# The ssm residual of blocks 2 to 6 by a second Strassen level, with LayerNorm's last small operations on VectorE and w2's second fold from SBUF

## The chip, the core and the metric

One core of a Trainium2 chip runs the kernel. The metric is the device time of one launch in microseconds (us); for the kernel before it is the median of three runs. The engines are TensorE (PE, with its weight loads as PEld), VectorE (DVE), ScalarE (ACT), GpSimd (POOL) and the sync engine (SP), which issues most of the DMAs.

## The reference

```python
emb = jnp.dot(jax.nn.silu(t), ada_w) + ada_b
shift_msa, scale_msa, gate_msa, shift_mlp, scale_mlp, gate_mlp = jnp.split(emb, 6, axis=-1)
norm = _ln(x) * (1.0 + scale_msa[:, None]) + shift_msa[:, None]
h = jax.nn.gelu(jnp.dot(norm, ssm_w1) + ssm_b1, approximate=False)
x = x + gate_msa[:, None] * (jnp.dot(h, ssm_w2) + ssm_b2)
norm2 = _ln(x) * (1.0 + scale_mlp[:, None]) + shift_mlp[:, None]
hf = jax.nn.gelu(jnp.dot(norm2, ff_w1) + ff_b1, approximate=True)
x = x + gate_mlp[:, None] * (jnp.dot(hf, ff_w2) + ff_b2)
```

x is (2, 2048, 512) in float32, t is (2, 512), ssm_w1 and ssm_w2 are 512 x 512, ff_w1 is 512 x 1024 and ff_w2 is 1024 x 512.

## The kernel before

x is cut into eight blocks of 512 tokens, four to each of the two batches. A block goes through LayerNorm 1 (`n1`), the product with ssm_w1 (hA), the product with ssm_w2 that is added to x (oA), LayerNorm 2 (`n2`), the product with ff_w1 (hC) and the product with ff_w2 that is added to x (oC). All weights stay in SBUF. The gates are multiplied into the columns of w2 and fw2 (a "fold"), once for each batch; for the second batch the weights are loaded again and folded again, while the kernel runs.

Every product is made by a fast scheme with fewer multiplications. hA and oA use Strassen's seven products P1 to P7; each is made of four matmuls of 128 x 128 by 256 columns and has a bank of PSUM: P1, P6, P7, P4 the bank "y", P2 "x", P5 and P3 "v". Sums of inputs that a product needs are made ahead on POOL. oC (`residual_in_leaves`, L761) carries Strassen one level further: P1 and P6 are plain products of eight matmuls, the others are cut into leaves, and a round R0 to R6 has ten matmuls of 128 columns, of leaf number n of five products. hC uses a scheme of its own (`products`, L955), whose inputs are 20 sums (`HK_B`, L915) made on POOL into the tile `forms`.

What a product adds to x, DVE adds from PSUM (L739 for oA, L789 and L838 for oC); for hidden layers L701 and L1002 are the like. A bank is used again and again, so an add that is late holds back the product that comes next in its bank. Where the next leaf value goes to the bank "x" too, ACT copies it there after R0 (L858 to L861).

LayerNorm takes statistics on DVE (L512, L513), then `scales` (L544) makes from mean and variance 1/sqrt (`pow`, on POOL, L550) and the scale and shift (`rstd`, `nmr`), by eight operations of 4 elements a partition on POOL. With them ACT writes the normalized rows (`normal`, L580), DVE transposes blocks of 32 (`turn`, L591), DMAs move the blocks (`move`, L600), and ACT scales and shifts (`moved`, L623).

The order on every engine is the order in the program: a product or round has hooks, and operations hung to a hook are issued right behind it. The loop over i = 1 to 7 issues, for i up to 4, hC_i, oA_(i+1), oC_i, hA_(i+2); for i = 5 (`ahead`) hC_5, oA_6, hA_7, oC_5, oA_7; then hC_6, oC_6, hC_7, oC_7. So the LayerNorm between oA_(i+1) and hC_(i+1) runs while oC_i is on PE, and n1 of block i + 2 runs while hC_i is on PE. The sums for oC_i (`sums24`, `sums35`, `sums7`, from L1023) are made on POOL during oA_(i+1) and at the start of oC_i. `leaf_fold` (i = 1 and 4) are sums of fw2 on DVE in oC. `refold2` (i = 2) reloads w2 in oC_2 and folds it in hA_4, with the gate that ACT copied to PSUM; `refold5` (i = 3) does the same with fw2.

The names that the steps of the prediction touch: `residual` L723, `residual_in_leaves` L761, `scales` L544, `weight_of_second` L391, `sums_of_first` L350 and `sums_of_second` L359 (four operations, all recorded at L348), `take_gate` L333, `load_gate` L328, `apart_leaves` L452, `gate_bias` L898.

Of the kernel before, what the change touches and what calls it, by code (L numbers as in the profile page):

```python
# [140 lines left out]
def kernel(  # L141
# [249 lines left out]
    def weight_of_second(w_sb, s, gt, engs, cut=1):  # L391
# [15 lines left out]
        return second_operands(q, s), ops + sums_of_second(q, s, nc.gpsimd, cut)  # L407
# [22 lines left out]

    Q = P // C
# [67 lines left out]
    class Norm:  # L499
# [44 lines left out]
        def scales(self, on_dve=False):  # L544

            n, v = self.name, nc.gpsimd
            ve = small.tile([P, C], F32, tag="ve", name=f"ve{n}")
            v.tensor_scalar(ve, self.mv[:, :, 1], self.of_squares, EPS, ALU.mult, ALU.add)
            r = small.tile([P, C], F32, tag="r", name=f"r{n}")
            v.tensor_tensor(r, ve, minus_half, ALU.pow)  # L550
            e = small.tile([P, C], F32, tag="e", name=f"e{n}")
            self.rstd = small.tile([P, C], F32, tag="rstd", name=f"rstd{n}")
            self.nmr = small.tile([P, C], F32, tag="nmr", name=f"nmr{n}")
            if on_dve:
                v = nc.vector
                v.tensor_tensor(e, r, ve, ALU.mult)
                v.scalar_tensor_tensor(e, e, -0.5, r, ALU.mult, ALU.mult)
                v.scalar_tensor_tensor(self.rstd, e, 1.5, r, ALU.add, ALU.mult)
                v.scalar_tensor_tensor(self.nmr, self.mv[:, :, 0], -1.0, self.rstd, ALU.mult, ALU.mult)
# [6 lines left out]
            v.tensor_scalar(self.nmr, self.nmr, -1.0, None, ALU.mult)  # L566
# [188 lines left out]

    LEAVES = ("P1", "P2", "P6", "P5", "P7", "P3", "P4")
# [737 lines left out]
```

## Time and profile before

| | |
|---|---|
| median of three runs | 586.56 us (586.24 to 586.59) |
| span of the profiled execution | 584.7 us |
| PE busy in the span | 577.8 us (99%) |
| DVE, ACT, POOL busy | 416.3, 263.2 and 428.2 us (71, 45 and 73%) |
| oA_3 on PE (223.10 to 235.18) | 12.1 us |
| oC_2 on PE (235.18 to 257.72) | 22.5 us |

A row of the timeline has the start in us from the span's start, the length in us, the engine, the line, the operation, out <- in with shapes and the number of instructions; in brackets stands the idle time of the engine before it and what ended it. A row of the groups ends with the busy time in us, the mean ns of one and the idle time before. A row of windows has the busy time of each engine in one stretch. The rows themselves stand in the prediction.

### The profile page before, as it was taken

How to read it: one execution, taken by the hardware profiler on the slowest of the kernel's cores; microseconds unless marked ns; L12 is line 12 of the kernel's file. 1: busy time of each engine (PE TensorE's matmuls, PEld its weight loads, DVE VectorE, ACT ScalarE, POOL GpSimd, SP SyncE). 2: the span in 40 equal slices, each digit the busy share in tenths (PEclk: the TensorE clock that was granted, in tenths of full speed). 3: DMA queues.
4: the chain of work that ended last, by engine and by line, in shares of the span. 5: the costliest groups of instructions: out<-in, count | busy, mean ns of one | idle time of the engine just before them, and what ended most of it. 6: DMA issues, size and time to landing. Idle time of an engine off the chain costs nothing.

```text
span 584.7 us, 9487 instructions
## 1 busy us (share of the span) xinstructions
PE 577.8 (99%) x3303; PEld 515.5 (88%) x3303; DVE 416.3 (71%) x752; ACT 263.2 (45%) x479; POOL 428.2 (73%) x518
## 2 busy tenths in 40 slices
PE   8999999999999999999999999999999999999997
PEld 4888888888889888998889988898888998899896
DVE  4978788987968375685756856884756367787676
ACT  2234357405642555435742588226673331731420
POOL 2875359999997938969788799998679445369351
PEclk9999999999999999999999999999999999999999
DMA  8990322303205403372043820244130330031002
GB/s 317 396 394 11 91 64 79 112 36 108 56 19 166 142 1 72 107 218 73 2 91 71 290 73 22 52 84 154 52 73 0 112 107 1 1 73 72 2 1 72
DMA packets 25243, 56.49 MB, mean 97 GB/s; under 512 B 4672, under 2 KB 5740, under 8 KB 23532
## 3 DMA queue, kind: packets, MB, share of 16 engines
q1 hardware_dynamic: 21856, 51.67, 27.9%
q10 hardware_dynamic: 3340, 4.22, 2.9%
q8 instruction: 26, 0.43, 0.3%
q14 instruction: 21, 0.17, 0.1%
HBM read 32.80 MB, written 8.40 MB: 70 GB/s over the span
## 4 chain that ended last, share of the span: by engine, by line
PE 93%; DMA 3%; DVE 2%; issue 0%; DVEq 0%
PE px_hC L985 10%; PE py_oA L475 9%; PE py_hA L475 9%; PE py_hC L985 8%; PE py_oC L778 8%; PE pv_hC L985 8%; PE pl_oC_P_y L824 8%; PE pv_oA L475 5%; PE pl_oC_P_v L824 5%; PE pv_hA L475 4%; PE pl_oC_P_x L824 3%; PE py_oC L475 2%; PE py_hC L475 2%; PE px_oA L475 2%; DMA ada<-in_L_cond_ada_w_dram 2%; PE px_hA L475 2%
## 5 line engine op out<-in xcount | busy, mean ns | idle before, releaser
L348 POOL TENSOR_TENSOR hSC<-hClo,hChi 128x512 f32<-128x512 f32 (+1 forms) x16 | 19.7, 1236 | 39.6 <-ACT hChi L980 34.2
L623 ACT ACTIVATE nT<-nT,mod,mod 128x512 f32<-128x512 f32 x32 | 23.4, 803 | 55.4 <-DMA nT<-blocks 39.8
L512 DVE BATCH_NORM_STATS2 st<-x 128x6 f32<-128x512 f32 x60 | 40.6, 678 | 5.4 <-DMA x<-in_x_dram 5.1
L923 POOL TENSOR_TENSOR forms<-forms 128x256 f32<-128x256 f32 x56 | 41.8, 747 | 3.3
L985 PE MATMUL py_hC<-forms,fw 128*128 128x256 f32 x168 | 41.0, 380 | 0.0
L1002 DVE TENSOR_TENSOR hClo<-hClo,py_hC 128x512 f32<-128x512 f32 x42 | 28.6, 684 | 15.3 <-ACT hClo L999 9.4
L985 PEld LDWEIGHTS py_hC<-forms,fw 128*128 128x128 f32 x168 | 31.7, 190 | 4.7 <-ACT hChi L999 0.2
L591 DVE STREAM_TRANSPOSE blocks<-nT 128x512 f32<-128x512 f32 x32 | 22.2, 705 | 13.5 <-ACT nT L580 13.5
L923 POOL TENSOR_TENSOR forms<-nT,forms 128x256 f32<-128x256 f32 x42 | 30.5, 748 | 1.7 <-PE pl_oC_P_v L824 1.3
L623 ACT ACTIVATE x<-x,mod,mod 128x512 f32<-128x512 f32 x24 | 17.6, 802 | 31.6 <-DMA x<-blocks 31.6
L923 POOL TENSOR_TENSOR forms<-nT 128x256 f32<-128x256 f32 x14 | 10.4, 741 | 28.4 <-ACT nT L623 18.0
L1002 DVE TENSOR_TENSOR hChi<-hChi,pv_hC 128x512 f32<-128x512 f32 x35 | 23.3, 681 | 10.4 <-PE pv_hC L985 6.7
L580 ACT ACTIVATE nT<-x,nmr,rstd 128x512 f32<-128x512 f32 x32 | 24.1, 806 | 13.3 <-POOL nmr L566 13.3
L985 PE MATMUL px_hC<-forms,fw 128*128 128x256 f32 x112 | 27.6, 379 | 0.0
L980 ACT ACTIVATE hClo<-hClo,colsT 128x256 f32<-128x256 f32 x56 | 25.3, 500 | 5.0 <-DVE hClo L1002 4.8
L838 DVE TENSOR_TENSOR x<-pl_oC_P_y,x 128x256 f32<-128x256 f32 (+1 forms) x66 | 24.7, 375 | 3.0 <-PE pl_oC_P_y L824 1.2
L475 PE MATMUL py_oA<-w,hA 128*128 128x256 f32 x112 | 26.5, 379 | 0.0
L999 ACT ACTIVATE hChi<-py_hC 128x512 f32<-128x512 f32 x14 | 7.6, 593 | 41.2 <-PE py_hC L985 41.0
L980 ACT ACTIVATE hChi<-hChi,colsT 128x256 f32<-128x256 f32 x56 | 25.1, 497 | 1.9 <-DVE hChi L1002 1.9
L739 DVE TENSOR_TENSOR x<-py_oA,x 128x512 f32<-128x512 f32 x26 | 17.8, 686 | 11.2 <-PE py_oA L475 10.6
L778 PE MATMUL py_oC<-fw_s,hSC 128*128 128x256 f32 x112 | 25.3, 379 | 0.0
L778 PE MATMUL py_oC<-fw,hClo 128*128 128x256 f32 x112 | 25.3, 379 | 0.0
(339 smaller groups left out, 1781.1 us busy)
## 6 DMA issues: line engine op xcount, KB each, us to landing
x<-in_x_dram SPq DMA_DIRECT2D x13, 1024.0 KB
out_dram<-x SPq DMA_DIRECT2D x14, 512.0 KB
ada<-in_L_cond_ada_w_dram SPq DMA_DIRECT2D x6, 1024.0 KB
x<-blocks SPq DMA_DIRECT2D x96, 64.0 KB
nT<-blocks SPq DMA_DIRECT2D x80, 64.0 KB
fw<-in_L_cond_ff_w_dram SPq DMA_DIRECT2D x2, 2048.0 KB
w<-in_L_cond_ssm_w_dram SPq DMA_DIRECT2D x3, 1024.0 KB
nT<-blocks ACTq DMA_DIRECT2D x48, 64.0 KB
```

The lines of the kernel that those rows point to most:

```text
L475: nc.tensor.matmul(ps[b][j * apart][:, j, :], lhs(p, j, k), rhs(p, j, k), start=(fresh and j * (not apart) == 0 and k == 0), stop=(p in (" ...
L512: nc.vector.bn_stats(st, xs[self.i][:, c, :])
L580: nc.scalar.activation(t, x_c, AF.Identity, bias=self.nmr[:, c : c + 1], scale=self.rstd[:, c : c + 1])
L591: nc.vector.transpose(self.bl[:, :, :, c, :].rearrange("p m k q -> p k m q"), self.nT[:, c, :].rearrange("p (k m q) -> p k m q", k=KD, m=C),)
L623: nc.scalar.activation(dst, src, AF.Identity, bias=shift, scale=scale)
L778: yield lambda j=j, k=k: nc.tensor.matmul(ps[BANK[p]][:, j, :], hops(p, j, k), wops[p][:, k, :], start=False, stop=(k == kdim - 1), skip_g ...
L824: nc.tensor.matmul(t[:, n, :], hops.leaves[p][f][:, k, :], leaf_wops[p][f][:, k, :], start=room not in started, stop=(f in ("P2", "P3", "P ...
L838: nc.vector.tensor_tensor(d, src, d, ALU.add)
L923: eng.tensor_tensor(reg[d], reg[a], reg[b], ALU.add if f == "+" else ALU.subtract)
L980: nc.scalar.activation(h, h, AF.Gelu_apprx_tanh, bias=fb1T[:, m : m + 1])
L985: nc.tensor.matmul(ps[b][:, j, :], fa[ra][:, j * P : (j + 1) * P], fb[rb].rearrange("p a (c q) -> p c a q", q=Q), start=(fresh and j == 0) ...
L1002: nc.vector.tensor_tensor(dest(d), dest(d), ps[b], op)
```

## The change

1. `residual_with_leaves` takes the place of `residual` for oA_2 to oA_6. P1, P5, P6 and P7 stay plain; P2, P3 and P4 are made in seven rounds of three matmuls 128 x 128 by 128 columns, in the order P1 R0 P5 R1 R2 P6 R3 R4 P7 R5 R6. Every plain product and every round but R0 is followed by its adds to x.
2. The sums that the leaves need: `leaf_sums` of hA (eight operations on POOL, at step 10 of hC) and `leaves_of_w2` (eight on POOL, ahead of the loop, and again at hA_4's P4). oA_7 takes the old form; `plain_w2` (two operations on DVE) gives it back its operands.
3. `scales` is cut in `root` and `rest`. For four early LayerNorms all stays on POOL. For the others `ve` and the four last operations are made on DVE, and `pow` alone on POOL. `root` and `rest` are hung to oC's P1 (n2), and to steps 2 and 12 of hC (n1; 0 and 9 at i = 1, 7 and 12 at i = 4, 0 and 2 at i = 5).
4. On POOL, sums24 is halved in oA; behind `pow` come the halves of sums35, sums7 and sums24 in turn.
5. w2's second fold reads the gate from a row in SBUF; four operations run in oC_2, four in hA_4, and its sums on DVE in place of POOL. The gate's copy in PSUM, for the bias alone, is taken at hA_4's P5. The loads of the gates are hung to oA in place of hC's first step, and `store_gates(2)` to hA_1's P7.
6. Tiles share memory: `w2_t` holds the identity matrix, silu and the gate rows early and the leaf sums of w2 later; the leaf sums of hA lie in a part of `forms`; `leaf_row` has two rows in place of three and two copies on ACT in place of one.

The diff, cut:

```diff
-    def weight_of_second(w_sb, s, gt, engs, cut=1):
+    def weight_of_second(w_sb, s, gt, engs, cut=1, sum_eng=nc.gpsimd):
...
+    def leaves_of_w2(w_sb, s, eng):
+
+        def views(w, n):
+            v = w.rearrange("p h (q e d) -> p h q e d", e=2, d=P)
+            return {f"{h + 1}{e + 1}": v[:, h, :, e] for h in range(2) for e in range(2)}
+
+        t23 = thirds(w2_t[:, : 6 * P].rearrange("p (s q d) -> p s q d", s=3, q=2))
+        t4 = thirds(w2_t[:, 6 * P :].rearrange("p (s q d) -> p s q d", s=3, q=1))
+        q23, q4 = views(w_sb[:, KD // 2 :, :], 2), views(s[:, 2], 1)
...
+        return ops, sums_of_second(q23, t23, eng) + sums_of_second(q4, t4, eng)
...
-        def scales(self, on_dve=False):
...
+        def scales(self):
+            self.root()
+            self.rest()
+
+        def root(self):
...
+            self.early = self.i + self.which in (2, 3)
+            v = nc.gpsimd if self.early else nc.vector
...
+            v.tensor_scalar(self.ve, self.mv[:, :, 1], self.of_squares, EPS, ALU.mult, ALU.add)
+            nc.gpsimd.tensor_tensor(self.r, self.ve, minus_half, ALU.pow)
+
+        def rest(self):
...
+            v = nc.vector
+            v.tensor_tensor(e, r, ve, ALU.mult)
+            v.scalar_tensor_tensor(e, e, -0.5, r, ALU.mult, ALU.mult)
+            v.scalar_tensor_tensor(self.rstd, e, 1.5, r, ALU.add, ALU.mult)
+            v.scalar_tensor_tensor(self.nmr, self.mv[:, :, 0], -1.0, self.rstd, ALU.mult, ALU.mult)
...
+    STEPS = ("P1", "R0", "P5", "R1", "R2", "P6", "R3", "R4", "P7", "R5", "R6")
+    STEP_OF = {"P1": "P1", "P2": "P5", "P6": "P6", "P5": "R4", "P7": "P7", "P3": "R5", "P4": "R6"}
+
+    def residual_with_leaves(name, i, hops, wops, leaf_wops, hooks):
...
+        def plain(p):
...
+            d = plain_dests[p]
+            nc.vector.tensor_tensor(d, ps[BANK[p]].unsqueeze(2).to_broadcast(d.shape), d, ALU.add)
+
+        def leaf_round(r):
+            f = LEAVES[r]
+            b = LEAF_BANK[f]
+            for n, p in enumerate(("P2", "P3", "P4")):
+                nc.tensor.matmul(
+                    rooms[b][:, n, :],
+                    hops.leaves[p][f],
+                    leaf_wops[p][f],
+                    start=b not in started,
+                    stop=(f in ("P2", "P3", "P4")),
+                    skip_group_check=True,
+                )
+                started.add(b)
+            if r == 0:
+                nc.scalar.copy(rooms["x"][:, :3], rooms["y"][:, :3])
+                started.add("x")
+                return
+            t, e = LEAF_AT[f]
+            for d, n in ((X[:, 0, t, :, e, :], slice(0, 2)), (X[:, 1, t, :1, e, :], slice(2, 3))):
+                nc.vector.tensor_tensor(d, rooms[b][:, n], d, ALU.add)
...
+        def leaf_sums(self, eng):
...
+            return sums_of_first(q24, s24, eng) + sums_of_first(q3, s3, eng)
...
-            hook(hooks, (0,), [n1[i + 2].scales])
+            hook(hooks, (0,), [n1[i + 2].root])
+            hook(hooks, (9,), [n1[i + 2].rest])
...
+            hook(hooks, (10,), hA[i + 1].leaf_sums(nc.gpsimd))
...
-            hook(hooks, (1,) if ahead else (7,) if unread_stats else (5,), [n1[i + 2].scales])
+            hook(hooks, (0,) if ahead else (7,) if unread_stats else (2,), [n1[i + 2].root])
+            hook(hooks, (2,) if ahead else (12,), [n1[i + 2].rest])
...
-            hook(hooks, ("P5",), sums24)
-        if fold:
-            sums35 = sums35[:2] + sums7[:2] + sums35[2:] + sums7[2:]
-        elif nx2:
-            hook(hooks, ("P7",), sums7)
+            hook(hooks, ("P5",), sums24[:2])
         if nx2:
...
+            sums35 = sums35[:2] + sums7[:2] + sums24[2:] + sums7[2:] + sums35[2:]
...
-            residual(f"oA_{i + 1}", i + 1, hA[i + 1], w2_ops, KD // 2, hooks, order=CARRIED)
...
+            residual_with_leaves(f"oA_{i + 1}", i + 1, hA[i + 1], w2_ops, w2_leaf, hooks)
...
-            if leaf_fold:
-                hook(hooks, ("P1",), leaf_fold[:2])
-            hook(hooks, ("P1",), [lambda: n2[i + 1].scales()])
+            hook(hooks, ("P1",), [lambda: n2[i + 1].root()])
+            hook(hooks, ("P1",), (leaf_fold or [])[:2] + [lambda: n2[i + 1].rest()])
             hook(hooks, ("P1",), sums35)
...
+            w2_ops, w2_fold = weight_of_second(w2_sb, w2_s, gate_rows[2, b], (nc.vector,), sum_eng=nc.vector)
+            hook(hooks, ("R2", "R4", "R4", "P3"), w2_fold[:KD])
...
-            take_gate(2, b)
-            w2_ops, w2_fold = weight_of_second(w2_sb, w2_s, gate[2, b], (nc.vector,))
-            hook(hooks, ALL, [multiply_2] + w2_fold)
...
+            hook(hooks, ("P1", "P1", "P2", "P6"), w2_fold[KD:])
+            hook(hooks, ("P5", "P4"), [lambda: found.update(gb2=bias_2()), lambda: found["gb2"]()])
+            w2_leaf, ops = leaves_of_w2(w2_sb, w2_s, nc.gpsimd)
+            hook(hooks, ("P4",), ops)
...
+            plain_w2(w2_sb, w2_s, nc.vector)
             residual(f"oA_{i + 2}", i + 2, hA[i + 2], w2_ops, KD // 2, hooks, order=CARRIED)
```

More of the change, by code (lines that the diff above doesn't have):

```diff
@@ new lines, in rest @@
+        def rest(self):
+            n, ve, r = self.name, self.ve, self.r
+            e, self.rstd, self.nmr = [small.tile([P, C], F32, tag=t, name=f"{t}{n}") for t in ("e", "rstd", "nmr")]
+            if self.early:
+                v = nc.gpsimd
+                v.tensor_tensor(e, r, r, ALU.mult)
+                v.tensor_tensor(e, e, ve, ALU.mult)
+                v.tensor_scalar(e, e, -0.5, 1.5, ALU.mult, ALU.add)
+                v.tensor_tensor(self.rstd, r, e, ALU.mult)
+                v.tensor_tensor(self.nmr, self.mv[:, :, 0], self.rstd, ALU.mult)
+                v.tensor_scalar(self.nmr, self.nmr, -1.0, None, ALU.mult)
+                return
+            v = nc.vector
[3 more added lines that the diff above has]
+            v.scalar_tensor_tensor(self.nmr, self.mv[:, :, 0], -1.0, self.rstd, ALU.mult, ALU.mult)
@@ L1274 @@
     fold = None
+    w2_leaf, ops = leaves_of_w2(w2_sb, w2_s, nc.gpsimd)
+    run(ops)
     later, unread_stats = [], []
```

144 lines of the change are left out of this document (90 added, 54 removed).

## The prediction

> **What bounds the kernel now.** I read the page from the top: busy time of the engines, then the chain that ended last.
>
> ```profile
> span 584.7 us, 9487 instructions
> PE 577.8 (99%) x3303; PEld 515.5 (88%) x3303; DVE 416.3 (71%) x752; ACT 263.2 (45%) x479; POOL 428.2 (73%) x518
> ...
> PE 93%; DMA 3%; DVE 2%; issue 0%; DVEq 0%
> ```
>
> PE is busy 99% of the span, and the chain of waits is PE for 93%. So two things move the time: matmul time that is added or taken away, and a new wait on PE. The profiled execution spans 584.7 us; the median of the runs is 586.56, so 1.86 us lie around the span, and I add that to every sum.
>
> The stretches of one regular block tell what the other engines have to spare (oA_3, oC_2, the most of hA_4; the last row is iteration i = 4 up to 406):
>
> ```profile
> core 0: us, PE busy (x) PEld busy (x) DVE busy (x) ACT busy (x) POOL busy (x), PEclk, DMA share, GB/s
> 223.26:235.35 12.09, 12.09 (x58) 10.64 (x57) 5.06 (x9) 4.60 (x11) 10.19 (x9) 1.00 0.42 101
> 235.35:257.88 22.53, 22.53 (x173) 21.70 (x173) 16.06 (x36) 9.62 (x16) 16.58 (x23) 1.00 0.50 146
> 257.88:268.25 10.37, 10.37 (x50) 9.13 (x49) 6.32 (x12) 5.01 (x9) 9.98 (x15) 1.00 0.39 126
> ...
> 337.00:406.00 69.00, 69.00 (x387) 62.13 (x387) 46.21 (x87) 38.95 (x79) 63.53 (x72) 1.00 0.27 77
> ```
>
> PE has no idle time there, and its granted clock (PEclk) is 1.00. The shares are of the stretch's own length. DVE has room in oA (5.06 of 12.09 us). POOL hasn't: 63.53 of 69.00 us in i = 4.
>
> **Part 1: P2, P3, P4 by leaves, on PE.** The chain of waits gives the cadence of both shapes.
>
> ```profile
> 154.10 1.73 PE py_oA L475 x8
> 175.33 2.23 PE pl_oC_P_x L824 x20
> ```
>
> A plain product is four matmuls of 256 columns in eight records: 1.73/4 = 0.432 us each. A leaf round in oC is ten matmuls of 128 columns in twenty records: 0.223 each. In each of oA_2 to oA_6, 12 matmuls of 256 (5.19 us) become 21 of 128 (4.69 us). That is 0.50 us less per block and 2.48 us in all: a span of 582.2 if PE waits for nothing new. oA then takes about 11.6 us in place of 12.09.
>
> **Part 2: more adds on DVE.** The groups of adds by shape:
>
> ```profile
> L739 DVE TENSOR_TENSOR x<-py_oA,x 128x512 f32<-128x512 f32 x26 | 17.8, 686 | 11.2 <-PE py_oA L475 10.6
> L838 DVE TENSOR_TENSOR x<-pl_oC_P_y,x 128x256 f32<-128x256 f32 x44 | 18.5, 420 | 1.6 <-DVE x L789 0.5
> L838 DVE TENSOR_TENSOR x<-pl_oC_P_y,x 128x128 f32<-128x128 f32 x22 | 6.2, 283 | 1.3 <-PE pl_oC_P_y L824 1.2
> 389.72 1.22 DVE L874 TENSOR_TENSOR x<-py_oC,x 128x1024 f32<-128x1024 f32 x1
> ...
> 235.18 3.62 PE L778 MATMUL py_oC<-fw,hClo 128*128 128x256 f32 x16
> ...
> 236.81 0.66 DVE L512 BATCH_NORM_STATS2 st<-x 128x6 f32<-128x512 f32 x1
> ...
> 237.61 0.66 DVE L512 BATCH_NORM_STATS2 st<-x 128x6 f32<-128x512 f32 x1
> ...
> 238.91 0.69 DVE L789 TENSOR_TENSOR x<-py_oC,x 128x512 f32<-128x512 f32 x1 [0.43 <-PE py_oC L778]
> ```
>
> Six adds of 512 (4.1 us) become two of 512, two of 1024 and six pairs of 256 and 128: 2 x 0.69 + 2 x 1.22 + 6 x 0.70 = 8.0 us. oA's 12.09 us hold the 3.9 us more, but the end of oA moves back on DVE. From T0, the start of oA: P7 ends at 11.60 - 2 x 0.67 = 10.26. An add starts 0.27 behind its product (oC_2's P1, two products long, ends at 235.18 + 3.46 = 238.64, its add starts at 238.91), so P7's runs from 10.53 to 11.75; the adds of R5 and R6 end at 13.15; the four statistics follow each other at 0.80 (236.81, 237.61) and end at 16.4; oC's P1 add ends at 17.0 and `ve`, now on DVE, at 17.2.
>
> **Part 3: the chain of LayerNorm.** In oC_2 before, with T0 = 223.10:
>
> ```profile
> 238.57 0.19 POOL L548 TENSOR_SCALAR ve<-mv 128x4 f32<-128x4 f32 x1 [0.61 <-DVE mv L513]
> 238.85 1.04 POOL L550 TENSOR_TENSOR r<-ve,minus_half 128x4 f32<-128x4 f32 x1
> 241.36 0.23 POOL L566 TENSOR_SCALAR nmr<-nmr 128x4 f32<-128x4 f32 x1
> 241.56 1.27 POOL L348 TENSOR_TENSOR forms<-hSC,hSC 128x512 f32<-128x512 f32 x1
> 241.62 1.52 ACT L580 ACTIVATE nT<-x,nmr,rstd 128x512 f32<-128x512 f32 x2 [3.92 <-POOL nmr L566]
> 243.05 0.36 ACT L858 COPY pl_oC_P_x<-pl_oC_P_y 128x256 f32<-128x256 f32 x1
> 244.32 0.61 PE L824 MATMUL pl_oC_P_x<-fw,hChi 128*128 128x128 f32 x4
> ```
>
> On ACT two normals stand ahead of the copy into the x bank, and round R1 on PE (244.32) starts from that copy, which ended at 243.41: 0.9 us of slack. nmr is ready at T0 + 18.5.
> After: `ve` 17.2, pow 1.04 to 18.2, four operations on DVE. The one place where DVE has done them:
>
> ```profile
> 9.79 0.16 DVE L556 TENSOR_TENSOR e<-r,ve 128x4 f32<-128x4 f32 x1 [0.93 <-POOL r L550]
> 10.38 0.16 DVE L559 SCALAR_TENSOR_TENSOR nmr<-mv,rstd 128x4 f32<-128x4 f32 x1
> ```
>
> 0.75 us for the four, so nmr at T0 + 19.0, normals to 20.5, copy to 20.8. PE wants R1 at 11.60 + 9.14 = 20.74 (R1 stands 244.32 - 235.18 = 9.14 behind oC's start). So in oC_2, oC_3 and oC_5 the slack is used up even when nothing disturbs DVE: about 0.1 us of stall each.
>
> **Part 4: DVE against POOL.** At 9.79 POOL was idle. In the changed order POOL goes from pow straight into 512-wide sums (sums35[:2], sums7[:2]), and each of the four operations reads both its inputs from SBUF. The trace shows what such neighbours do to each other:
>
> ```profile
> 154.74 1.56 DVE L348 TENSOR_TENSOR fw_t<-fw_s 128x256 f32<-128x256 f32 x1
> 156.34 1.38 DVE L348 TENSOR_TENSOR fw_t<-fw_s,fw_t 128x256 f32<-128x256 f32 x1
> ...
> 170.81 0.42 DVE L348 TENSOR_TENSOR fw_t<-fw,fw_t 128x256 f32<-128x256 f32 x1
> ...
> 154.75 1.27 POOL L348 TENSOR_TENSOR hSC<-hChi,hSC 128x512 f32<-128x512 f32 x1
> 155.98 1.45 POOL L348 TENSOR_TENSOR hSC<-hClo,hChi 128x512 f32<-128x512 f32 x1
> ```
>
> A 256-wide operation that takes 0.42 us alone takes 1.56 and 1.38 beside POOL's sums. It ends 0.28 us behind the end of POOL's operation (156.02), and the next one has to wait for POOL's next (157.43): they alternate. The adds with a PSUM operand show nothing of it (420 and 686 ns are means over the whole run). [...]
>
> No row shows a four-element DVE operation against a busy POOL. The nearest are POOL's own tiny ones against DVE:
>
> ```profile
> 446.46 0.54 POOL L548 TENSOR_SCALAR ve<-mv 128x4 f32<-128x4 f32 x1 [0.62 <-DVE mv L513]
> 447.08 1.36 POOL L550 TENSOR_TENSOR r<-ve,minus_half 128x4 f32<-128x4 f32 x1
> 446.29 0.66 DVE L348 TENSOR_TENSOR x<-x 128x512 f32<-128x512 f32 x1
> 446.86 0.68 DVE L348 TENSOR_TENSOR nS<-x,nS 128x512 f32<-128x512 f32 x1
> ```
>
> There each lost 0.35 and 0.32 us to the operation in flight (0.19 and 1.04 undisturbed, quoted above). Bounds for a chain: from below 0; from above four operations behind four of POOL's, 2 x 1.27 + 2 x 0.73, some 3.5 to 4 us. By the nearest rows a tiny operation loses about a third of a microsecond, which makes 4 x 0.33 = 1.3 us in a chain, one POOL operation. I take 1.3 us.
>
> What that costs PE, site by site. oC_2 and oC_3: 1.3 + 0.1 = 1.35 us each, since R1 waits for it directly. oC_5: with hA_7's products between oA_6 and it, most of the chain runs ahead of its R1; I take a third, 0.45. oC_1 and oC_4: all normals stand behind the copies on ACT, so R1 isn't reached through them, but DVE is held and the adds queued behind the chain come late (P6's, R1's and R2's, and PE's R4 waits for R2's): about 0.7 for the chain in oC_1, 1.2 in oC_4. And the second part of the leaf operations (`leaf_fold`) ran beside POOL's tiny operations before and now runs beside its sums:
>
> ```profile
> 378.09 1.06 DVE L348 TENSOR_TENSOR fw_s<-fw_s 128x256 f32<-128x256 f32 x1
> ...
> 377.60 1.27 POOL L348 TENSOR_TENSOR forms<-hChi,forms 128x512 f32<-128x512 f32 x1
> ```
>
> Three such operations, at 0.65 us more each as at 378.09 or up to 1.1 as at 154.74, hold DVE some 2 us longer in oC_4 (2.0 on PE, 3.2 with the chain); in oC_1 I take 0.3 (1.0 with the chain), since DVE has less to do there. hC_5, where `rest` comes at step 2 while POOL sums: DVE's adds free the banks of the following products, 1.6. Elsewhere in hC `rest` comes at step 12, where nothing but the next add waits for DVE; I take 0. Sum: oC_1 1.0, oC_2 1.35, oC_3 1.35, oC_4 3.2, hC_5 1.6, oC_5 0.45 = 8.95 us. With two or three POOL operations in a chain in place of one the same list gives 2.7 + 2.4 + 2.4 + 5.0 + 2.5 + 1.4 = 16.4.
>
> **Part 5: more on POOL.**
>
> ```profile
> 235.06 0.72 POOL L348 TENSOR_TENSOR forms<-hClo 128x256 f32<-128x256 f32 x1
> ```
>
> leaf_sums of hA is four sums 256 wide and four 128 wide: from 4 x 0.72 = 2.9 to 8 x 0.72 = 5.8 us; I take 4.7 per block. Six tiny operations leave (from pow's end, 238.85 + 1.04, to 241.59: 1.7 us). Net +3 us in a 69 us iteration that has 5.5 to spare in i = 4. It falls at step 10 of hC, ahead of sums that aren't due before oA; POOL then ends its last s35 sums some 0.2 us ahead of the round that reads them. At 0 here, up to 1 us in all for the range.
>
> **Part 6: w2's second fold.**
>
> ```profile
> L396 DVE TENSOR_TENSOR w<-w,pgate 128x512 f32<-128x512 f32 x8 | 5.1, 676 | 0.0
> ```
>
> Of the folds, four now run in oC_2, with the gate from SBUF and not from PSUM: 0.68 us each alone, up to 1.27 more beside POOL's sums. They stand behind the adds of R3 and R5 on DVE. The first products of hA_4 (5.2 us at 1.73 each) cover them, and hA_4's P5 waits only for R5's last add, which stands ahead of the folds. On SP's queue the loads of the gate rows move from the first step of hC into oA (P2 and P7), behind nothing that PE waits for, and `store_gates(2)` comes an iteration earlier than its rows are read. On POOL the four sums of w_s leave for DVE, where hA_4 has room (6.32 of 10.37 us are busy there), and the eight leaf sums of w2 come (4.7 us) ahead of hC_3's end. I take 0, and up to 1.5 us if R6's adds become the wait.
>
> **The sum.** 584.7 - 2.48 + 8.95 = 591.2 span, + 1.86 = 593.0 us.
>
> **Rivals.**
> *No contention for tiny operations, leaf operations alone suffer.* oC_4 2.0, oC_1 0.3, hC_5 0.4, three times 0.1: 3.0 us of stall eats the 2.48: 584.7 - 2.48 + 3.0 + 1.86 = 587.1, about the same as before. For it: the tiny operations read 16 bytes a partition. Against: 446.46.
> *No contention that reaches PE.* Only the 0.1 us at R1: 584.7 - 2.48 + 0.4 + 1.86 = 584.5, faster. For it: PE has hardly a wait now, and DVE's 71% leaves room. Against: rows 154.74 and 378.09, and that R1's slack is gone on paper.
> *Full alternation.* Every operation of a chain waits for one of POOL's, as the pair 154.74 and 156.34 did: 16.4 us and more, 584.7 - 2.48 + 16.4 + 1.86 = 600.5, or 605 with 3.5 us at each site. It decides from the point where a chain takes over 2 us from pow's end to nmr. For it: that row pair. Against: a tiny operation may slip in between two of POOL's. [...]
>
> **How the numbers follow.** What a measurement can tell from no change is 0.2%, 1.2 us: below 585.4 is faster, above 587.7 slower. Forecast (one POOL operation per chain, 588 to 597): 0.36. Full alternation: 0.21. Leaf operations alone: 0.13, of which 0.10 within 0.2% and 0.03 above. No contention on PE's path: 0.30. So faster 0.30, same 0.10, slower 0.36 + 0.21 + 0.03 = 0.60. The range takes in the side without stalls down to 584.0 (584.5 less the half microsecond that the small terms may be off) and full alternation up to 602; what is left out is about 0.1 at each end. The likeliest case's own is 588 to 597.
>
> **What would show it.** Right: in oC_2 the row of `e` on DVE lasts 0.5 us or more in place of 0.16, from pow's end to nmr it is about 2 us, and PE waits ahead of R1 for ACT's copy. Right for part 1: oA_3 spans 11.6 us. Wrong: the four operations at 0.16 each beside sums of 1.27, no new PE idle time, and a span near 582.5. A PE wait on POOL's sums (s35 or leaf_sums) or on a DMA of the gate would be a cause that I don't price.

## The result and the profile after

The changed kernel takes 619.25 us (median of four runs, 618.2 to 622.77) against 586.58 for the kernel before on the same chip: a ratio of 1.057 (95% interval 1.054 to 1.060), 32.7 us slower. The forecast was 593.0 with a range up to 602: the right direction, and far too little. All ratios here are of fast runs: beside x4, x5 and x6 two of the seven runs of the kernel before were slow (672.12 and 1238.8 us) and are left out of them.

The page of the changed kernel, with the lines that answer to those of before:

```profile
span 616.6 us, 9778 instructions
PE 588.4 (95%) x3393; PEld 521.2 (85%) x3393; DVE 476.0 (77%) x865; ACT 263.8 (43%) x486; POOL 438.3 (71%) x491
...
PE 59%; DVE 13%; POOL 9%; issue 8%; ACT 5%; DMA 4%; ACTq 1%; SPq 0%; DVEq 0%; POOLq 0%
```

The chain that ended last was PE for 93%; now DVE, POOL and ACT hold a quarter of it. Two things are to be seen: PE has 616.6 - 588.4 = 28.2 us without work (6.9 before), and its busy time rose by 10.6 us though it has fewer columns to multiply. What PE waited for most in the changed kernel (us in total, times, longest):

```profile
PE py_hC L1091 <- DVE hClo L1108: 8.7, 3, 5.3
PE pl_oC_P_x L916 <- ACT pl_oC_P_x L950: 5.4, 3, 2.0
PE pl_oC_P_y L916 <- DVE x L930: 3.0, 1, 3.0
PE px_hC L1091 <- ACT hClo L1105: 2.2, 2, 1.6
```

From the first matmul of each stage in the timelines of PE, a table of the stages follows: length before and difference to it, in us, for the changed kernel and for the experiments told below (stages that differ nowhere by over 0.3 us are left out).

| stage | before | after | x1 | x2 | x6 | x8 | x7 | x11 |
|---|---|---|---|---|---|---|---|---|
| hC_1 | 22.46 | +2.27 | +0.17 | +7.09 | +1.56 | +2.28 | +0.02 | 0 |
| oA_2 | 12.08 | -0.24 | -0.49 | 0 | -0.49 | -0.26 | -0.49 | -0.48 |
| oC_1 | 22.54 | +0.98 | +4.77 | +3.74 | +1.01 | +0.60 | 0 | 0 |
| oA_3 | 12.08 | -0.49 | -0.48 | 0 | -0.49 | -0.49 | -0.49 | -0.49 |
| oC_2 | 22.54 | +3.93 | +0.46 | +1.42 | +2.30 | +0.24 | 0 | 0 |
| hA_4 | 12.09 | 0 | 0 | 0 | +0.51 | +0.35 | 0 | 0 |
| hC_3 | 22.45 | +3.79 | +2.83 | +7.02 | +1.89 | +6.12 | +0.61 | +0.19 |
| oA_4 | 12.08 | -0.49 | -0.48 | 0 | -0.49 | -0.48 | -0.49 | -0.48 |
| oC_3 | 22.54 | +2.30 | +0.48 | +1.42 | +3.94 | +0.25 | 0 | 0 |
| hA_5 | 12.09 | +1.13 | +0.69 | +0.88 | 0 | +0.36 | +1.90 | 0 |
| hC_4 | 22.70 | +9.34 | -0.06 | +12.15 | +1.64 | +9.15 | -0.06 | +0.14 |
| oA_5 | 12.09 | 0 | -0.46 | 0 | -0.50 | 0 | -0.49 | 0 |
| oC_4 | 22.54 | +4.85 | +4.57 | +3.05 | +4.57 | +1.22 | +4.65 | +0.44 |
| hC_5 | 22.52 | +2.21 | 0 | +5.35 | 0 | +2.88 | +0.30 | +0.22 |
| oA_6 | 12.09 | -0.49 | -0.50 | 0 | -0.50 | -0.50 | -0.50 | -0.50 |
| oC_5 | 22.54 | +2.37 | 0 | 0 | +2.34 | +0.16 | 0 | 0 |
| hC_6 | 22.45 | +0.15 | 0 | +2.12 | +0.15 | +0.15 | +0.15 | +0.15 |

In the column "after" the oA stages show what part 1 brings: 0.49 us where nothing disturbs it. The stages hC lose 17.8 us, oC 14.4.

Now the place where the prediction looked, oC_2, in the timeline of the changed kernel (DVE, POOL, ACT, PE; T0, oA_3's start, is 226.28):

```profile
242.72 0.16 DVE L574 TENSOR_SCALAR ve<-mv 128x4 f32<-128x4 f32 x1
244.01 1.22 DVE L591 TENSOR_TENSOR e<-r,ve 128x4 f32<-128x4 f32 x1 [1.13 <-POOL r L575]
245.27 0.16 DVE L592 SCALAR_TENSOR_TENSOR e<-e,r 128x4 f32<-128x4 f32 x1
245.47 1.12 DVE L593 SCALAR_TENSOR_TENSOR rstd<-e,r 128x4 f32<-128x4 f32 x1
246.63 0.65 DVE L594 SCALAR_TENSOR_TENSOR nmr<-mv,rstd 128x4 f32<-128x4 f32 x1
...
242.96 1.02 POOL L575 TENSOR_TENSOR r<-ve,minus_half 128x4 f32<-128x4 f32 x1 [7.01 <-DVE ve L574]
243.95 1.26 POOL L349 TENSOR_TENSOR forms<-hSC,hSC 128x512 f32<-128x512 f32 x1
245.30 1.27 POOL L349 TENSOR_TENSOR forms<-forms,hSC 128x512 f32<-128x512 f32 x1
...
247.37 1.52 ACT L608 ACTIVATE nT<-x,nmr,rstd 128x512 f32<-128x512 f32 x2 [4.42 <-DVE nmr L594]
248.79 0.36 ACT L950 COPY pl_oC_P_x<-pl_oC_P_y 128x256 f32<-128x256 f32 x1
...
249.21 0.92 PE L916 MATMUL pl_oC_P_x<-fw,hChi 128*128 128x128 f32 x4 [2.03 <-ACT pl_oC_P_x L950]
249.92 1.06 PE L916 MATMUL pl_oC_P_x<-fw,hSC 128*128 128x128 f32 x4
```

POOL goes from pow straight into its sums (243.95). `e` takes 1.22 us and ends 0.02 us behind POOL's first sum; the second operation slips in before POOL's next one (0.16); `rstd` and `nmr` wait again. From pow's end (243.98) to nmr (247.28) it is 3.3 us in place of 0.75. The normals, the copy and R1 follow one behind the other, and PE waits 2.03 us. And then the four matmuls of the next record take 1.06 where the same record took 0.61 before: PE runs at half speed. The windows of the changed kernel show the granted clock:

```profile
core 0: us, PE busy (x) PEld busy (x) DVE busy (x) ACT busy (x) POOL busy (x), PEclk, DMA share, GB/s
246.16:249.57 3.41, 1.38 (x8) 0.93 (x7) 2.43 (x4) 2.17 (x5) 3.33 (x5) 1.00 0.00 0
249.57:252.98 3.41, 3.41 (x19) 3.41 (x18) 1.78 (x4) 1.56 (x3) 3.41 (x4) 0.50 0.00 0
252.98:256.40 3.42, 3.42 (x32) 3.42 (x32) 2.75 (x8) 0.00 (x0) 3.34 (x4) 1.00 0.86 201
```

So a wait of 2.03 us cost oC_2 3.93 us: PE ran 3.41 us at a clock of 0.50, which is 1.7 us. In oC_3 the same wait (at 323.57, also 2.03 us) left the clock at 1.00 and cost 2.30. The largest loss is at a place that the prediction put at nothing, step 12 of hC_4:

```profile
365.54 0.98 DVE L591 TENSOR_TENSOR e<-r,ve 128x4 f32<-128x4 f32 x1
366.55 2.27 DVE L592 SCALAR_TENSOR_TENSOR e<-e,r 128x4 f32<-128x4 f32 x1
368.85 2.26 DVE L593 SCALAR_TENSOR_TENSOR rstd<-e,r 128x4 f32<-128x4 f32 x1
371.15 0.65 DVE L594 SCALAR_TENSOR_TENSOR nmr<-mv,rstd 128x4 f32<-128x4 f32 x1
371.72 0.68 DVE L1108 TENSOR_TENSOR hClo<-hClo,py_hC 128x512 f32<-128x512 f32 x1
372.43 0.60 ACT L1105 ACTIVATE hClo<-py_hC 128x512 f32<-128x512 f32 x1 [6.97 <-DVE hClo L1108]
373.06 0.69 DVE L1108 TENSOR_TENSOR hClo<-hClo,py_hC 128x512 f32<-128x512 f32 x1 [0.66 <-ACT hClo L1105]
...
366.44 2.36 POOL L349 TENSOR_TENSOR fw<-fw 128x1024 f32<-128x1024 f32 x1
368.74 2.35 POOL L349 TENSOR_TENSOR fw_s<-fw,fw_s 128x1024 f32<-128x1024 f32 x1
...
373.80 3.78 PE L1091 MATMUL py_hC<-forms,fw 128*128 128x256 f32 x8 [5.26 <-DVE hClo L1108]
```

POOL's sums are 1024 wide here, the second and the third of the four operations each wait for a whole one and end 0.02 us behind it, and hClo's add at 371.72 stands behind the four. ACT's operation waits for that add, and a second add (373.06) for ACT's. It ends at 373.75; PE, which waited 5.26 us for the bank that it reads, goes on at 373.80; the next eight records take 3.78 us in place of 1.89, at half the clock.

### The profile page after: what moved, and what is told of

Same layout as the page of the kernel before. It is cut to its first block, busy times and chain, and to the rows that moved or that the text cites. A ratio compares the mean times of both kernels' runs of the same rounds, so it can differ in the third digit from the quotient of the medians.

```text
span 616.6 us, 9778 instructions
## 1 busy us (share of the span) xinstructions
PE 588.4 (95%) x3393; PEld 521.2 (85%) x3393; DVE 476.0 (77%) x865; ACT 263.8 (43%) x486; POOL 438.3 (71%) x491
## 4 chain that ended last, share of the span: by engine, by line
PE 59%; DVE 13%; POOL 9%; issue 8%; ACT 5%; DMA 4%; ACTq 1%; SPq 0%; DVEq 0%; POOLq 0%
PE py_hA L495 7%; PE px_hC L1091 7%; PE py_hC L1091 6%; PE pv_hC L1091 5%; PE pl_oC_P_y L916 4%; PE py_oA L495 3%; PE pv_hA L495 3%; POOL hSC L349 3%; PE pl_oC_P_v L916 3%; PE py_oC L869 3%; DVE x L930 2%; PE py_hC L495 2%; PE py_oC L495 2%; POOL forms L1015 2%; POOL forms L349 2%
## 5 line engine op out<-in xcount | busy, mean ns | idle before, releaser
L575 POOL TENSOR_TENSOR r<-ve,minus_half 128x4 f32<-128x4 f32 x16 | 16.6, 1037 | 54.0 <-DVE ve L574 34.0
L1091 PE MATMUL py_hC<-forms,fw 128*128 128x256 f32 x168 | 43.5, 395 | 8.7 <-DVE hClo L1108 8.7
L1091 PEld LDWEIGHTS py_hC<-forms,fw 128*128 128x128 f32 x168 | 32.5, 197 | 15.2 <-DVE hClo L1108 10.6
L1015 POOL TENSOR_TENSOR forms<-nT,forms 128x256 f32<-128x256 f32 x42 | 31.8, 777 | 0.5
L1105 ACT ACTIVATE hClo<-px_hC 128x512 f32<-128x512 f32 x21 | 12.5, 596 | 31.5 <-PE px_hC L1091 18.8
L1091 PE MATMUL px_hC<-forms,fw_s 128*128 128x256 f32 x84 | 21.9, 390 | 3.5 <-ACT hClo L1105 2.2
L349 POOL TENSOR_TENSOR hClo<-hClo 128x512 f32<-128x512 f32 (+1 forms) x23 | 25.1, 1094 | 0.0
```

The costliest lines, as they stand in the source:

```text
L349: eng.tensor_tensor(out[:, r], a[:, r], b[:, r], f)
L1015: eng.tensor_tensor(reg[d], reg[a], reg[b], ALU.add if f == "+" else ALU.subtract)
L1091: nc.tensor.matmul(ps[b][:, j, :], fa[ra][:, j * P : (j + 1) * P], fb[rb].rearrange("p a (c q) -> p c a q", q=Q), start=(fresh and j == 0) ...
```

## The experiments

Theory A is that DVE's four-element operations wait for POOL's sums since both their inputs come from SBUF. Theory B is the longer queue of DVE and POOL from the leaves. Theory C is about the clock behind a wait. Each run's ratio is to the kernel before on the same chip.

**x1: the small operations back on POOL.** In the changed kernel:

```diff
-            self.early = self.i + self.which in (2, 3)
+            self.early = self.i + self.which != 1
...
-            hook(hooks, (0,) if ahead else (7,) if unread_stats else (2,), [n1[i + 2].root])
-            hook(hooks, (2,) if ahead else (12,), [n1[i + 2].rest])
+            hook(hooks, (1,) if ahead else (7,) if unread_stats else (5,), [n1[i + 2].scales])
```

> The changed kernel with its third part undone: every LayerNorm's small operations (but the first one's) back on POOL, at the hooks of the kernel before. Theory A (DVE's four-element operations wait for POOL's sums, and all that stands behind them on DVE and ACT is late): the waits of PE in hC_3, hC_4 and hC_5 and ahead of R1 in oC_2, oC_3 and oC_5 go, at least 20 of the 32 us come back, 586 to 598 us. Theory B (the longer queue of adds on DVE from the leaves, and POOL's leaf sums, make the chain late whoever computes it): less than 10 us come back, over 609 us.

Measured: 599.45 us, ratio 1.023 (1.021 to 1.024). 19.8 us come back, a little under the 20 that theory A asked for, and the time lies 1.45 us above its range. What remains has other places: hC_1, hC_4, hC_5 and oC_5 are as before, oC_2 and oC_3 lose 0.5, but oC_1 and oC_4 lose 4.8 and 4.6, now to POOL, and hC_3 2.8 (DVE waits 2.08 us there for w2's bias row, and the small operations come late on POOL). Theory A explains the larger part and not the rest.

**x2: the kernel before with the four operations on DVE.**

```diff
         def scales(self, on_dve=False):
 
+            on_dve = on_dve or self.i + self.which not in (2, 3)
```

> The kernel before with the four last operations of the same LayerNorms on VectorE in place of six on POOL, at the places of the kernel before, and nothing else. Theory A: the first of the four lasts 1.2 us in place of 0.16 where POOL goes straight into sums, nmr is 1 to 3 us later than its 18.5 us behind the start of oA, and PE waits where it didn't: 592 to 612 us. Theory B: DVE has room in this kernel, the four take 0.75 us and the time is 585.5 to 588.

Measured: 631.85 us, ratio 1.078 (1.075 to 1.080), beyond what either theory gave. With no leaves at all the four operations at these places cost 45 us. Not all of it is contention: in hC_3 and hC_4 of this kernel DVE stands still for pow as well, since here the four operations follow it at once (timeline of DVE in x2):

```profile
295.43 0.16 DVE L557 TENSOR_TENSOR e<-r,ve 128x4 f32<-128x4 f32 x1 [7.24 <-POOL r L551]
...
372.30 2.30 DVE L557 TENSOR_TENSOR e<-r,ve 128x4 f32<-128x4 f32 x1 [4.39 <-POOL r L551]
374.63 2.26 DVE L558 SCALAR_TENSOR_TENSOR e<-e,r 128x4 f32<-128x4 f32 x1
```

At 295.43 POOL has nothing to do behind pow, and the operation takes 0.16 us; at 372.30 POOL sums, and it takes 2.30. What the root, ten steps ahead of the rest, spares the changed kernel is the 7.24 and the 4.39 (0.48 us and none there), not the contention.

**x3: longer work on ACT ahead of R1, in the kernel before.**

```diff
+            if i in (2, 3, 5):
+                hook(hooks, ("P1",), [lambda: n2[i + 1].normal(1)] * {2: 2, 3: 3, 5: 4}[i])
```

> The kernel before with one LayerNorm row block normalized again on ScalarE (the same values, 0.76 us each) ahead of the copy that R1 waits for: two more in oC_2, three in oC_3, four in oC_5. With 0.9 us of slack PE should wait 0.6, 1.4 and 2.1 us. Theory C (a wait of PE of some length is followed by some microseconds at half the granted clock, so that it costs nearly twice its length): oC_5 is longer by 2.1 + about 1.9 us, oC_3 in between, oC_2 by 0.6 alone, and the granted clock falls to 0.5 to 0.9 behind the longer waits. Rival (the slow stretch in the changed kernel came from something else in it): each stage is longer by its wait alone, 4.1 us in all, and the clock stays at 1.00.

Measured: 590.2 us, a single run. PE waits 0.69 and 1.54 us in oC_2 and oC_3, these are 0.96 and 1.81 us longer, and the clock stays at 1.00. oC_5 is unchanged: its chain of LayerNorm ends so early there that the copy, at 465.3, still stands 2.6 us ahead of R1. So the long wait that this run was to bring didn't come about: it shows that a wait of up to 1.54 us costs 0.27 us more than itself, and leaves theory C open. The traces of x6 and of the changed kernel take it up in the last section.

**x4 and x5: what holds oC_1 and oC_4 in x1.** x4 is x1 without hA's leaf sums in these two iterations, x5 is x1 with the sums for oC in the old order.

```diff
-            hook(hooks, (10,), hA[i + 1].leaf_sums(nc.gpsimd))
+            hA_leaf_sums = hA[i + 1].leaf_sums(nc.gpsimd)
+            if i not in (1, 4):
+                hook(hooks, (10,), hA_leaf_sums)
```

> The kernel of x1 (small operations back on POOL) with the leaf sums of hA left out at i = 1 and i = 4, so that the leaves of oA_2 and oA_5 multiply other data. In x1, oC_1 and oC_4 are 4.8 and 4.6 us longer than before, waiting for POOL's sums. Theory D (POOL has no room for 4.65 us more in these two iterations): both come back by at least 3 us each, 590 to 594 us. Theory E (the new order of sums24, sums7 and sums35 behind pow makes them late): both stay, 598 to 601 us.

```diff
-            hook(hooks, ("P5",), sums24[:2])
+            hook(hooks, ("P5",), sums24)
...
-            sums35 = sums35[:2] + sums7[:2] + sums24[2:] + sums7[2:] + sums35[2:]
+        if i in (1, 4):
+            sums35 = sums35[:2] + sums7[:2] + sums35[2:] + sums7[2:]
+        elif nx2:
+            hook(hooks, ("P7",), sums7)
```

> The kernel of x1 with POOL's sums for oC in the order of the kernel before (sums24 whole and sums7 ahead of pow). Theory E: oC_1 and oC_4 come back to within 1 us of before, 589 to 592 us. Theory D: POOL's end is no earlier, the two stages keep 3 us or more each, 597 to 602 us.

Measured: x4 592.84 us (ratio 1.011, 1.009 to 1.013), oC_1 +0.62 and oC_4 +0.99 in place of +4.77 and +4.57. x5 604.77 us (1.031, 1.028 to 1.033), oC_1 +8.04 and oC_4 +7.23, so the time lies above theory D's 597 to 602. Theory D holds for both stages, as x4 shows: POOL has no room for the leaf sums at i = 1 and 4. The new order is no cause but a help, since it takes pow ahead of two sums.

**x6: one operand of each tiny operation in PSUM.** In the changed kernel, for n1 alone, so in hC:

```diff
+            self.in_psum = self.which == 1 and self.i > 2
+            if self.in_psum:
+                self.pw = ps_t.tile([P, D], F32, tag="t", name=f"pw{n}")
+                nc.vector.tensor_copy(self.pw[:, :C], self.ve)
+                nc.vector.tensor_copy(self.pw[:, C : 2 * C], self.mv[:, :, 0])
...
+            if self.in_psum:
+                ve, mean, e = [self.pw[:, k * C : (k + 1) * C] for k in range(3)]
```

> The changed kernel with one operand of each of the four operations of n1 (the ones in hC_1 to hC_5) in PSUM in place of SBUF, by two small copies behind ve; the same operations, places and order, and POOL as it was. Theory A (what counts is that both inputs come from SBUF): each of the four lasts 0.15 to 0.2 us in hC_1, hC_3, hC_4 and hC_5 although POOL sums beside them, these four stages come back by 10 to 17 us in all, 602 to 609 us; the operations in oC stay slow. Rival (DVE is slow there for another reason, such as its queue or the semaphores between the two engines): they stay at 0.65 to 2.3 us and the time at 617 to 622 us.

Measured: 604.11 us, ratio 1.030 (1.028 to 1.032). The same step 12 of hC_4 in the timeline of x6, beside the same kind of sums on POOL:

```profile
361.88 0.16 DVE L598 TENSOR_TENSOR pw<-r,pw 128x4 f32<-128x4 f32 x1
362.07 0.17 DVE L599 SCALAR_TENSOR_TENSOR pw<-pw,r 128x4 f32<-128x4 f32 x1
362.27 0.16 DVE L600 SCALAR_TENSOR_TENSOR rstd<-pw,r 128x4 f32<-128x4 f32 x1
362.47 0.16 DVE L601 SCALAR_TENSOR_TENSOR nmr<-pw,rstd 128x4 f32<-128x4 f32 x1
...
360.08 2.35 POOL L349 TENSOR_TENSOR fw_s<-fw,fw_s 128x1024 f32<-128x1024 f32 x1
362.40 2.35 POOL L349 TENSOR_TENSOR fw<-fw 128x1024 f32<-128x1024 f32 x1
```

0.75 us for the four, while POOL goes from one 1024-wide sum into the next. hC_4 comes from +9.34 to +1.64, hC_5 from +2.21 to 0, the four stages by 12.5 us. Same operations, same places, same POOL: in hC theory A is shown, and DVE's queue or the semaphores are not the cause. What the four stages keep, 5.1 us, wasn't told apart; `ve` still takes 2.02 us in hC_4. The rows of oC are slow as before.

**x8: POOL held until nmr is done.** In the changed kernel, behind the four operations of oC:

```diff
+        def hold(self):
+            t = small.tile([P, C], F32, tag="hold", name=f"hold{self.name}")
+            nc.gpsimd.tensor_scalar(t, self.nmr, 1.0, None, ALU.mult)
...
-            hook(hooks, ("P1",), (leaf_fold or [])[:2] + [lambda: n2[i + 1].rest()])
+            hook(hooks, ("P1",), (leaf_fold or [])[:2] + [lambda: n2[i + 1].rest(), lambda: n2[i + 1].hold()])
```

> The changed kernel with one more four-element operation on POOL in each oC, which reads nmr and stands behind the four operations in the program: POOL's sums behind pow can't start until DVE has done them. Nothing else is changed, hC neither. Theory A: in oC the four last 0.16 us each, nmr is ready 0.8 us behind pow in place of 3.3, and the waits ahead of R1 in oC_2, oC_3 and oC_5 shrink to under 0.6 us; with what the clock lost behind them 6 to 12 us come back, 607 to 613 us. Rival (POOL's sums are late already, and holding them moves the waits to PE's rounds that read them): oC's stages stay within 1 us of the changed kernel's, 617 us or more.

Measured: 608.61 us, ratio 1.038 (1.035 to 1.041). The timeline of x8 in oC_4:

```profile
398.33 0.16 DVE L591 TENSOR_TENSOR e<-r,ve 128x4 f32<-128x4 f32 x1 [0.57 <-POOL r L575]
398.53 0.16 DVE L592 SCALAR_TENSOR_TENSOR e<-e,r 128x4 f32<-128x4 f32 x1
398.73 0.16 DVE L593 SCALAR_TENSOR_TENSOR rstd<-e,r 128x4 f32<-128x4 f32 x1
398.92 0.16 DVE L594 SCALAR_TENSOR_TENSOR nmr<-mv,rstd 128x4 f32<-128x4 f32 x1
399.00 0.42 DVE L349 TENSOR_TENSOR fw_t<-fw 128x256 f32<-128x256 f32 x1
399.45 0.42 DVE L349 TENSOR_TENSOR fw_t<-fw,fw_t 128x256 f32<-128x256 f32 x1
399.80 1.49 DVE L349 TENSOR_TENSOR fw<-fw 128x256 f32<-128x256 f32 x1
...
399.17 0.33 POOL L598 TENSOR_SCALAR hold<-nmr 128x4 f32<-128x4 f32 x1 [0.87 <-DVE nmr L594]
399.48 1.53 POOL L349 TENSOR_TENSOR forms<-hSC,hSC 128x512 f32<-128x512 f32 x1
```

With POOL still, all four take 0.16, and the leaf operations behind them 0.42 until POOL starts again (1.49). oC_2 to oC_5 come from +3.93, +2.30, +4.85 and +2.37 to +0.24, +0.25, +1.22 and +0.16. It cost POOL 0.9 us of rest, and no wait of PE in oC over 0.7. hC_3 got longer by it (+6.12): POOL is later there, DVE waits 2.44 us for pow at step 12 and then for three sums.

**x7, x9, x10, x11: everything mended.** x7 has the remedies of x6 and x8 (ve for n1 on POOL), the sums for oC ahead of pow, all normals behind the copies for R1, w2's leaf sums in hC_0 and at step 10 of hC_3, and w2's bias row loaded four products earlier. x9 takes the changed kernel's order of sums at i = 4 again and issues the load of x's block 6 behind fw2's. x10 leaves oA_5 plain, x11 is x10 with the switch of w2's operands on POOL, and at step 10 of hC in place of 17.

```diff
-    w2_leaf, ops = leaves_of_w2(w2_sb, w2_s, nc.gpsimd)
-    run(ops)
...
+    hook(hooks, ("P2",), ops)
...
-            hook(hooks, ("R0",) if leaf_fold else ("P1", "P1", "R0"), [lambda c=c: n2[i + 1].normal(c) for c in range(C)])
+            hook(hooks, ("R0",), [lambda c=c: n2[i + 1].normal(c) for c in range(C)])
```

> The changed kernel with every found cost mended: n1's operations with one operand in PSUM and ve on POOL, POOL held in oC as in x8, sums24 and sums7 ahead of pow as before, all normals behind the copies for R1, w2's leaf sums in hC_0 and behind hA's leaf sums in hC_3, w2's bias row loaded four products earlier. If the list of causes is complete, the 2.45 us of part 1 are left, less what POOL and leaf_fold still cost in oC_1 and oC_4 (up to 3 us): 584 to 588 us. If something else slows the changed kernel, it shows as PE waits at other places and a time over 590 us.

> The kernel of x7 with its two remaining losses mended: at i = 4 the order of POOL's sums is the changed kernel's (pow stands ahead of the second half of sums24, since POOL has no pause there in x7), and the load of x's block 6 is issued behind fw2's second load and not ahead of it, since DVE waits for that load in hA_5 (PE 1.7 us). If these are the causes, oC_4 comes from +4.65 to about +1.2 us, as in x8, and hA_5 from +1.9 to under 0.5: 584.5 to 586.8 us, at or below the kernel before. If x's block, now later, holds ACT's statistics, hA_5 or hC_4 keep 1 us or more and the time is 587 to 590.

```diff
-                hook(hooks, (10,), hA[i + 1].leaf_sums(nc.gpsimd) + w2_later)
+            if i != 4:
+                hook(hooks, (10,), hA[i + 1].leaf_sums(nc.gpsimd) + w2_later)
+            if i in (4, 5):
+                hook(hooks, (17,), [lambda: plain_w2(w2_sb, w2_s, nc.vector)])
```

> The kernel of x9 with oA_5 by plain products again (no leaf sums of hA at i = 4; four small operations on DVE bring w2's operands to the plain form and back). In x9 only oC_4 is still long (+2.4 us), with POOL busy from hA_5 to oC_4. If POOL's 4.65 us there are the cause, oC_4 comes to under +0.7 us, oA_5 costs 0.5 us again, and the time falls by 1.0 to 1.5 us to 586.0 to 586.8, level with the kernel before. If DVE's leaf operations beside POOL's sums are the cause, oC_4 keeps 1.5 us or more and the time is 587.3 to 588.3.

```diff
-                hook(hooks, (17,), [lambda: plain_w2(w2_sb, w2_s, nc.vector)])
+                hook(hooks, (10,), [lambda: plain_w2(w2_sb, w2_s, nc.gpsimd)])
```

> The kernel of x10 with the four small operations that bring w2's operands to the plain form and back on POOL (1.2 us each time, where its 4.65 us of leaf sums are gone) in place of DVE. In x10 they cost hC_4 1.7 and hC_5 1.0 us. Theory A (on DVE, with both inputs in SBUF, they waited for POOL's sums and held the adds): both go to under 0.3 us, the span to about 583.6 and the time to 585.0 to 586.8, at or below the kernel before. If POOL is late by them, hC_4 or oC_4 keep 1 us: 587 to 588.5.

Measured: x7 590.12 us (ratio 1.006, 1.005 to 1.008), x9 587.64 (1.002, 1.001 to 1.003), x10 589.57 (1.005, 1.004 to 1.007), x11 586.64 (1.0005, 0.9996 to 1.0014). x7 misses its 584 to 588: oC_4 (+4.65) and hA_5 (+1.90) stayed, the first by the order of sums with POOL full, the second since DVE waits for fw2's load. x9 lies just over its range: hA_5 came to 0, but oC_4 kept 2.4. x10 brings oC_4 to +0.45, as was expected if POOL's load is the cause there too (DVE has fewer adds in oA_5 as well, which wasn't told apart), but its time misses both of its ranges: it pays in hC_4 (+1.7) and hC_5 (+1.0), where two operations with both inputs in SBUF stand on DVE. x11 moves these to POOL and both are gone. The profiled execution of x11 spans 584.1 us against 584.7, and the runs can't tell it from the kernel before: none of the versions beats it.

## Why the prediction was wrong

*Part 1* was right: 0.49 us per oA stage, 11.59 in place of 12.08, where 0.50 and 11.6 were forecast.

*Part 2* was nearly right in its order: P7's add, the rounds' adds, statistics and `ve` on DVE one behind the other, only R6's adds among the statistics. `ve` ended at T0 + 16.6 and pow at T0 + 17.7, where 17.2 and 18.2 were forecast.

*Part 4* named the mechanism and mis-sized it. The step that failed first is the choice of 1.3 us per chain, taken from POOL's tiny operations beside DVE. Measured in oC_2 it is 3.3 - 0.75 = 2.55 us, twice that: DVE's operations fall in line with POOL's, three of four waited (1.22, 1.12 and 0.65 us in place of 0.16). The row pair 154.74 and 156.34, quoted for the rival "full alternation", was the nearer one. That rival's condition (over 2 us from pow's end to nmr) is met. Its list of 16.4 us is close to what its six places lost together, 16.6 where the forecast had 8.95. oC_3, oC_4 and hC_5 came near it one by one (2.30, 4.85 and 2.21 for 2.4, 5.0 and 2.5, oC_4 with the clock in it); that oC_1, oC_2 and oC_5 (0.98, 3.93 and 2.37 for 2.7, 2.4 and 1.4) make up for each other is luck.

The step that failed worst is "Elsewhere in hC `rest` comes at step 12, where nothing but the next add waits for DVE; I take 0". hC_1, hC_3 and hC_4 lost 2.27, 3.79 and 9.34 us, 15.4 of the 32. (In hC_1 `rest` stands at step 9.) The next add is what frees the bank of a following product, so PE waits for it (5.26 us in hC_4); and POOL's sums there are up to 1024 wide, so the wait is by POOL's operation (2.27 and 2.26 us beside sums of 2.36 and 2.35), not by DVE's. x6 shows it: hC_1, hC_3 and hC_4 together come from 15.4 to 5.1. Not all of it is by these operations: hC_3 keeps 2.83 with them on POOL (x1), and hC_1 1.56 in x6. Full alternation stayed at 600.5 to 605 for the same reason: it took nothing at these places either.

What stood nowhere in the prediction is the clock. At the waits of 2.03 us in oC_2, 5.26 in hC_4 and 2.99 in oC_4 the clock went to 0.50 (249.57 to 252.98, 372.45 to 379.28 and 416.82 to 420.23). The view of the cores gives the mean of the changed kernel (1.000 before):

```profile
core 0: 616.6 us, clock 0.987
```

That is (1 - 0.987) x 616.6 = 8.0 us of clock. What fell in PE's work is 3.41 us, 5.48 (from 373.80, where the wait ends) and 3.41 at half speed: 6.2 us lost. PE's busy time rose by 10.6 us where 21 matmuls in place of 12 should have taken some 2.5 us off it, so the clock is about half of that rise; the runs don't place the rest. oC_2 was forecast at 1.35, its wait was 2.03, and it cost 3.93.

The other terms of the sum: oC_1 1.0 against 0.98, oC_3 1.35 against 2.30, oC_4 3.2 against 4.85, hC_5 1.6 against 2.21, oC_5 0.45 against 2.37. oC_5's "a third" had no ground: its R1 waited 1.38 us for the same copy as in oC_2.

*Part 5* was right at i = 1 and too low at i = 4, though the changed kernel hides it. With the small operations on POOL, x1 and x4 show that the leaf sums at i = 1 and 4 cost 4.2 and 3.6 us. With them on DVE oC_1 loses nothing (x7), but oC_4 keeps 2.4 us in x9 and 0.46 without the leaves of oA_5 (x10), with POOL held for nmr in both: 5.5 us of room in 69 is not enough there, where the sums that PE reads come at the end of it.

*Part 6* was nearly right for the folds (hA_4 is 12.09 us as before), and wrong for the bias row: its load is issued at hA_4's P5 and DVE stands still for it in hC_3, with statistics and adds behind it, a wait of the kind that x7 mends by an earlier load (it mended others in hC_3 with it, and their shares weren't told apart):

```profile
278.05 0.69 DVE L994 TENSOR_TENSOR gb<-pgate,gb 128x512 f32<-128x512 f32 x1 [1.58 <-DMA gb<-in_L_cond_ssm_b_dram]
```

A size of 16 bytes a partition is no protection: in hC_4 of the changed kernel an operation of that size takes up to 2.27 us beside POOL's sums with both inputs in SBUF, and 0.16 or 0.17 with one in PSUM (x6).

## What to carry to other kernels

A small operation is not cheap by its size: with both inputs in SBUF, DVE's four-element operation took 0.16 us beside a still POOL and up to 2.27 beside POOL's sums in the changed kernel, and in a chain of four two to four of them waited. Look at where each operand lives, and put one in PSUM (0.16 to 0.17 us each in x6), or keep the other engine still for the length of the chain (0.16 each in x8). When a price goes from an engine off the path to an engine in order, ask what stands behind it there: in hC_4 PE waited 5.26 us for a bank behind one late add. And a wait of TensorE can cost nearly twice its length (2.03 us cost 3.93 in oC_2), since the clock can fall behind it (0.50 for 3.41 us there).

## What was not expected of the hardware

The clock behind a wait depends on more than the wait's length. In x6, R1 waits 2.03 us in oC_2 (from 245.90) and 2.04 us in oC_3 (from 319.27). The clock of x6 around the two:

```profile
243.59:247.00 3.41, 2.31 (x11) 1.70 (x9) 2.37 (x5) 0.91 (x2) 3.25 (x5) 1.00 0.00 0
247.00:250.42 3.42, 2.49 (x22) 2.49 (x23) 2.59 (x4) 2.83 (x6) 3.42 (x4) 1.00 0.00 0
250.42:253.83 3.41, 3.41 (x33) 3.41 (x32) 3.06 (x9) 0.00 (x0) 3.41 (x4) 1.00 0.53 120
...
318.68:322.10 3.42, 1.38 (x10) 0.98 (x9) 2.08 (x4) 2.60 (x6) 3.34 (x4) 1.00 0.00 0
322.10:325.51 3.41, 3.41 (x19) 3.41 (x18) 1.95 (x4) 1.13 (x2) 3.41 (x5) 0.50 0.08 19
```

The same wait ahead of the same round leaves the clock at 1.00 in oC_2 (+2.30 us in all) and takes it to 0.50 in oC_3 (+3.94). In the changed kernel the stretches at 0.50 last 3.41, 6.83 and 3.41 us, and they start at 249.57, 372.45 and 416.82, which are 36 and 13 times 3.413 us apart.

Windows of 3.413 us, laid over a trace so that its clock changes at their ends, tell the cases apart. In oC_2 of x6 the wait falls into two windows, 1.11 us and 0.93; in oC_3 it lies in one. In the changed kernel it is the other way round: the wait of 2.03 us lies in one window in oC_2, with the clock at 0.50 behind it, and falls into two in oC_3, 1.09 us and 0.94, with the clock at 1.00. In the changed kernel, from 12 us on, every window at full clock in which PE was idle for 1.56 us or less was followed by full clock, and the three with more (2.03 us from 246.16, 3.41 from 369.04 and 2.02 from 413.41) by half. No window of this trace lies between 1.56 and 2.02. That was read from waits that happened, and no run sets it on purpose.

An operation with one input in SBUF waited as well: `ve` in hC_4 of the changed kernel, beside a 1024-wide sum of POOL.

```profile
360.83 2.22 DVE L574 TENSOR_SCALAR ve<-mv 128x4 f32<-128x4 f32 x1 [0.97 <-ACT unread L555]
...
360.67 2.35 POOL L349 TENSOR_TENSOR fw_s<-fw 128x1024 f32<-128x1024 f32 x1
```

It ends 0.03 us behind POOL's sum; at 242.72, where POOL had nothing to do, the same operation took 0.16. What sets it apart from the operations of x6 that have an input in PSUM and took 0.16 us beside such sums, no run shows.
